# Fills of K on GpSimd, gates among the first maxima, and a reordered join between the stages of a two-layer network

## The chip, the cores and the metric

The kernel runs on one core of a Trainium2 chip. A core has five engines with queues of their own: TensorE (PE, matrix products and transposes), VectorE (DVE), ScalarE (ACT), GpSimd (POOL) and SyncE (SP, which here only issues transfers). The metric is the device time of one execution in microseconds (us). Time before: 1257.92 us, the median of three runs (1256.42 to 1259.0).

## The reference

The input is one sequence of 2048 tokens with 128 channels. Two layers follow each other. Each has an attention part and a feed-forward part, each in front of a gate and behind a layer norm whose scale and shift come from a small vector `c` through `wmod`:

```python
mod = (_silu(c) @ wmod).reshape(1, 6, 1, -1)
sa, ca, ga, sb, cb, gb = ...                       # six rows of 128
ga = (2 * (ga >= 0) - 1) * jnp.maximum(jnp.abs(ga), 0.25)      # gb alike
h = _layernorm(x) * (1 + ca) + sa;  x = x + ga * attention(h)
h = _layernorm(x) * (1 + cb) + sb;  x = x + gb * feed_forward(h)
```

- Layer 0's attention has 16 heads of 8 channels, with biases on all projections, and no mask.
- Layer 0's feed-forward adds a shared part (SiLU-gated, 512 wide) to the product of one expert of 16 per token, picked by the largest router logit and weighted by its sigmoid.
- Layer 1's attention has 8 query heads of 16 channels on one common key and value head, causal.
- Layer 1's feed-forward mixes each token with the one before it and gates a squared ReLU with a sigmoid.

## The kernel before

**Blocks.** The 2048 tokens lie in four query blocks of 512 (`QB`), each of four row tiles of 128 (`TB`). `x` stays in SBUF through both layers.

**Start.** `first_norm` normalises the four blocks: statistics on VectorE (L632, L633), the root on ScalarE (L635), the normalisation on VectorE (L228), four transposes on TensorE (L235) and the eviction with scale and shift on ScalarE (L236) into `hT`. Its PSUM pool is closed before the attention's is opened, so the attention's first product (`pq`, L676) needs the last eviction.

**Layer 0's attention.** A head's keys and queries are split into a high and a low half and stacked in rows, so that one product with 64 rows gives the score of two halves each. K's stack `kS0` has eight slices of 2048 columns. Each slice is first filled with a pattern (`fill`, L658: rows 31, 63, 95 and 127 are one, the others zero; the column `last_rows`, L97, holds it), then four transfers write the halves into part of its rows (`stack`, L259, from SP's queue, for the first two slices from ScalarE's too). The rows of ones serve to add the query's negative maximum to the score: the stack of queries gets that maximum in its rows 31, 63, 95 and 127.

**Units, two passes.** A unit is one query block and one group of four heads; there are 16. Its first pass (`first_pass`) makes 32 score tiles (L380, three PSUM buffers of 128 x 1024) and takes their maxima on VectorE (L384). At its end `largest` gathers the maxima (L395, L405, L406) and `turn` transposes them (L413), copies them (L414) and sends them into the query stack (L417). The second pass (`second_pass`) makes the scores again the other way round (L445), takes the exponential on ScalarE (L455) and weighs the values (L471).

**What sets the order.** The second pass of unit u and the first pass of the units after it are recorded alternately: `look_ahead` keeps the first passes a lead of `LEAD` = 8 steps in front. A turn waits in `turns` until two more steps are recorded. `late` holds pieces (normalising, projecting, routing) that are taken one at a time between the steps of a second pass; layer 0's list begins with `fold0`, which makes layer 1's modulation (L109) and gates (L121 to L126), folds gates into weights (L800, L802, L275, L277) and adds the output bias to `x` on GpSimd (L284). Up to the end of layer 0's attention a scheduler orders each engine's instructions from what is recorded; `keep_in_program_order` pins one of them.

**Join after layer 0's attention.** `last0` writes out an order by hand (from there on TensorE, VectorE and ScalarE keep the order of the program): the last projection, the shared part of the first block (`up` L869, `silu` L874, `times` L878, `down` L882, `add` L889), and the last block's routing (`choose`, `place`, `send`). `tiles` (L825 to L851) computes on VectorE which expert each tile of sorted tokens belongs to; SP's and TensorE's registers are loaded from its result `nth_i`, and SP then gathers the tokens (`xs`, L999).

**Experts, and the join before layer 1's attention.** Eight groups of expert tiles run with slices of the shared part of blocks 1 to 3 between them (`shared_step`: `shared_up` L972, `shared_act` L946 and L952, `shared_down` L960). After the last, tokens' expert rows are fetched by GpSimd (L1077) and added (L1091); blocks 0 and 1 are normalised (`moments`, L180 to L195, L228), and layer 1's keys and queries are made (L264).

Of the kernel before, what the change touches and what calls it, by code (L numbers as in the profile page):

```python
# [10 lines left out]
F32 = mybir.dt.float32  # L11
# [3 lines left out]
AF = mybir.ActivationFunctionType  # L15
# [28 lines left out]
def two_layers(ctx: ExitStack, tc: tile.TileContext, a: dict, out: bass.AP):  # L44
# [46 lines left out]
    def vcol(i, n=1):  # L91
        return vec[:, i:i + n]
# [3 lines left out]
    last_rows = const.tile([P, 1], F32, name="last_rows")  # L96
    nc.vector.tensor_reduce(last_rows, ident[:, 31::32], AX.X, ALU.add)  # L97

# [4 lines left out]

    def modulation(layer, ps):
        if layer == 0:
            nc.scalar.activation(sg, vcol(V_C0, 2), AF.Sigmoid)
            nc.vector.tensor_mul(sc, sg, vcol(V_C0, 2))
        for j in range(6):
            nc.tensor.matmul(ps[:, j:j + 1], wmod[layer][:, j * P:(j + 1) * P],  # L109
                             sc[:, layer:layer + 1], start=True, stop=True)  # L110
# [61 lines left out]

    def statistics(b, name):
# [9 lines left out]
        return mv, [lambda: some(0, TB // 2), lambda: some(TB // 2, TB)]  # L183

    def moments(b, name, root=False, between=lambda: None):


        mv, steps = statistics(b, name)
        for step in steps:
            step()  # L190
# [95 lines left out]
    def attention(layer, hT, ngrp, dk, scale, causal, kvp, begin, prepare, wq, bq, folded, ended,  # L286
# [23 lines left out]
        with ExitStack() as s:  # L310
# [36 lines left out]
            def project_q(b):  # L347
                if b in qS:
                    return
                ps = other_bank()  # L350
                nc.tensor.matmul(ps, wq, hT[:, b * QB:(b + 1) * QB], start=True, stop=True)
                hi = kvp.tile([P, QB], F32R, name=f"{L}qh{b}", tag="qh")
# [14 lines left out]
            def first_pass(u):  # L367
# [5 lines left out]
                def step(i, kb, pair):  # L373
# [9 lines left out]
                    if not own:  # L383
                        nc.vector.tensor_reduce(pm[:, i, 2 * pair:2 * pair + 2, kb], ps,  # L384
                                                AX.X, ALU.max)
                    for j in range(2 if own else 0):
# [37 lines left out]
                last = steps.pop()  # L424
                return steps + [lambda: (last(), largest(), turns.append([0, turn]))]

# [118 lines left out]
            shift, late, turns, weights, ready = {}, [], [], [], []  # L545
            if not folded:
                late.append(lambda: folded.extend(fold0(other_bank())))

            def all_first():
                for u in range(len(units)):  # L550
# [3 lines left out]
                    for i, step in enumerate(first_pass(u)):  # L554
# [3 lines left out]
                        if not fused and (grp, i) == (0, int(b > 0)) and b + 1 < NB:  # L558
                            ready.extend(prepare(b + 1, other_bank))
                            ready.insert(len(ready) - 1, lambda b=b: project_q(b + 1))  # L560
                        step()
                        if ready:
                            ready.pop(0)()
# [23 lines left out]

            short = 0 if fused else LEAD - 3
            look_ahead(ends[0] + LEAD - short)
# [66 lines left out]
    def fill(st):  # L656

        nc.scalar.activation(kS0[:, st, :], last_rows.to_broadcast([P, T]), AF.Copy)  # L658

# [5 lines left out]
    def begin0(ep, pp, stacks):  # L665
# [4 lines left out]
        vA = pool.tile([P, NT, (H0 - 1) * VW + W], F32, name="vA0", tag="vA")  # L670
        nc.gpsimd.memset(vA[:, :, H0 * VW:], 0.0)

        qhi = pool.tile([P, QB], F32R, name="a0qh0", tag="qh")
# [15 lines left out]
        for st in range(nst):  # L689
            rows = slice(st * 2 * D0, (st + 1) * 2 * D0)  # L690
            queues = (nc.sync, nc.scalar) if st < 2 else (nc.sync,)
            if st >= 2:
                fill(st)
            stack(kS[:, st, :], (hi[rows], lo[rows]), (0, 1, 0, 1), queues, RT // D0)
            stack(stacks[0][:, st, :], (qhi[rows], qlo[rows]), (0, 0, 1, 1), queues, RT // D0)
        for b in range(NB):
            for pair in range(TB // 2):
                ps = pp.tile([P, 2, QB], F32, name=f"pv{b}{pair}", tag="s")
                for j in range(2):
# [6 lines left out]
                    bv0.unsqueeze(1).to_broadcast([P, 2, H0 * VW]), ALU.add)  # L706
        gates(0)
        return ((lambda st: kS[:, st, :]),
                (lambda kt, head: vA[:, kt, head * VW:head * VW + W]), stacks[0])
# [113 lines left out]

    def tiles():

# [29 lines left out]
    def last0(late, bank, ps_s, ep):  # L855
# [41 lines left out]
        def rows():  # L897
# [30 lines left out]
    with ExitStack() as s:  # L928
# [159 lines left out]

        def add(b):
            ts = slice(b * TB, (b + 1) * TB)  # L1090
            return nc.vector.tensor_tensor(x[:, ts, :], x[:, ts, :], yx[:, ts, :], ALU.add)  # L1091
# [262 lines left out]
```

## Time and profile before

| | |
|---|---|
| Median of the runs | 1257.92 us (1256.42 to 1259.0) |
| The profiled execution | 1246.13 us, span 1244.4 us |
| TensorE busy | 1155.9 us, 93% of the span |
| VectorE busy | 951.9 us, 76% |
| ScalarE busy | 774.2 us, 62% |
| GpSimd busy | 85.9 us, 7% |
| Mean granted TensorE clock | 0.946 |

The span runs from the first to the last instruction of one execution. The rows by slice cut it into 40 equal parts of 31.1 us and give each engine's busy share in tenths. The chain of waits is followed back from the last instruction: each line has its start in us, its length in us, the engine, the tile written, the line of the kernel, and how many instructions it merges. A line of a group has engine, operation, output and input, shapes and count, then busy us and mean ns of one, then the idle time before it. A line of one tile's instructions gives the shortest, the middle and the longest duration in ns, and the first and last start.

### The profile page before, as it was taken

How to read it: one execution, taken by the hardware profiler on the slowest of the kernel's cores; microseconds unless marked ns; L12 is line 12 of the kernel's file. 1: busy time of each engine (PE TensorE's matmuls, PEld its weight loads, DVE VectorE, ACT ScalarE, POOL GpSimd, SP SyncE). 2: the span in 40 equal slices, each digit the busy share in tenths (PEclk: the TensorE clock that was granted, in tenths of full speed). 3: DMA queues.
4: the chain of work that ended last, by engine and by line, in shares of the span. 5: the costliest groups of instructions: out<-in, count | busy, mean ns of one | idle time of the engine just before them, and what ended most of it. 6: DMA issues, size and time to landing. Idle time of an engine off the chain costs nothing.

```text
span 1244.4 us, 22459 instructions
## 1 busy us (share of the span) xinstructions
PE 1155.9 (93%) x9264; PEld 527.9 (42%) x9264; DVE 951.9 (76%) x1515; ACT 774.2 (62%) x845; POOL 85.9 (7%) x152
## 2 busy tenths in 40 slices
PE   4679999999999999999999999979977999999995
PEld 2333433434443444343343443437744444444443
DVE  3788898899898889889889884243368699898532
ACT  6107777777777777777777778752333355656763
POOL 2002000000000000000000000230141111100111
PEclk9558999999999999999999999998987799999997
DMA  4841010202220212210000000032210101000000
GB/s 123 113 51 35 2 53 1 70 27 77 70 70 2 69 33 77 64 53 2 1 2 2 2 2 2 18 116 76 66 38 24 32 3 35 1 1 1 2 18 17
DMA packets 63110, 45.22 MB, mean 36 GB/s; under 512 B 6624, under 2 KB 56928, under 8 KB 62496
## 3 DMA queue, kind: packets, MB, share of 16 engines
q1 hardware_dynamic: 60240, 40.37, 13.2%
q10 hardware_dynamic: 1744, 1.32, 0.6%
q0 software_dynamic: 1024, 2.10, 0.6%
q8 instruction: 73, 1.20, 0.4%
q14 instruction: 29, 0.24, 0.1%
HBM read 9.88 MB, written 21.95 MB: 26 GB/s over the span
## 4 chain that ended last, share of the span: by engine, by line
PE 81%; DVE 12%; ACT 4%; DMA 1%; issue 1%; SPq 0%; DVEq 0%; ACTq 0%; POOLq 0%; POOL 0%
PE a0bank L471 24%; PE a0p L445 17%; PE a0p L380 13%; PE a1bank L471 5%; PE a1p L445 4%; DVE a0mx L384 3%; DVE a1mx L384 3%; PE a1p L380 2%; PE a1p L451 2%; DVE a1masked L389 2%; PE sg L972 2%; ACT a0e L455 1%; PE gu L1024 1%; PE a0bank L509 1%; PE sum L960 1%
## 5 line engine op out<-in xcount | busy, mean ns | idle before, releaser
L384 DVE TENSOR_REDUCE a0mx<-a0p 128x2 f32<-128x1024 f32 x512 | 623.8, 1224 | 74.6 <-PE a0p L380 64.9
L455 ACT ACTIVATE a0e<-a0p 128x1024 f32<-128x1024 f32 x512 | 522.6, 1025 | 171.5 <-PE a0p L445 146.4
L471 PE MATMUL a0bank<-a0e,vA 128*32 128x256 f32 x4096 | 333.3, 391 | 0.8 <-ACT a0e L455 0.8
L380 PE MATMUL a0p<-kS,a0qS 64*128 64x512 f32 x1024 | 248.0, 480 | 23.6 <-DVE a0mx L384 13.1
L445 PE MATMUL a0p<-a0qS,kS 64*128 64x512 f32 x1024 | 260.5, 497 | 0.0
L455 ACT ACTIVATE a1e<-a1p 128x1024 f32<-128x1024 f32 (+3 forms) x160 | 143.2, 897 | 108.5 <-PE a1p L451 103.0
L445 PEld LDWEIGHTS a0p<-a0qS,kS 64*128 64x128 f32 x1024 | 97.3, 184 | 204.5 <-issue 129.5
L380 PEld LDWEIGHTS a0p<-kS,a0qS 64*128 64x128 f32 x1024 | 100.3, 192 | 108.4 <-ACT a0e L455 56.8
L471 PEld LDWEIGHTS a0bank<-a0e,vA 128*32 128x32 f32 x4096 | 86.3, 108 | 137.4 <-issue 123.8
L384 DVE TENSOR_REDUCE a1mx<-a1p 128x2 f32<-128x1024 f32 x96 | 115.7, 1220 | 14.8 <-PE a1p L380 14.4
L471 PE MATMUL a1bank<-a1e,vA 128*32 128x256 f32 (+1 forms) x1152 | 97.1, 385 | 0.4 <-POOL a1e L458 0.4
L445 PE MATMUL a1p<-a1qS,kS 64*128 64x512 f32 (+3 forms) x320 | 76.6, 465 | 5.4 <-DVE a1mx L384 4.2
L380 PE MATMUL a1p<-kS,a1qS 64*128 64x512 f32 (+3 forms) x320 | 67.8, 423 | 11.5 <-DVE a1mx L389 4.6
L389 DVE CUSTOM_DVE_ANT_0 a1masked<-a1p,later 128x128 f32<-128x128 f32 (+3 forms) x128 | 62.4, 487 | 11.7 <-PE a1p L380 6.2
L780 POOL DMA_INDIRECT sent<-hs,row_i x16 | 15.8, 988 | 712.4 <-DVE ln11xn L228 689.2
L451 PE MATMUL a1p<-a1mT,a1ones 64*128 64x512 f32 (+3 forms) x320 | 61.7, 375 | 0.0
L445 PEld LDWEIGHTS a1p<-a1qS,kS 64*128 64x128 f32 x320 | 31.5, 189 | 63.3 <-issue 24.8
L380 PEld LDWEIGHTS a1p<-kS,a1qS 64*128 64x128 f32 x320 | 32.2, 195 | 39.9 <-DVE a1mx L389 11.6
L471 PEld LDWEIGHTS a1bank<-a1e,vA 128*32 128x32 f32 x1152 | 25.7, 108 | 42.5 <-issue 35.2
L458 POOL TENSOR_SCALAR_AFFINE_SELECT a1e<-a1e 128x256 f32<-128x256 f32 x64 | 26.1, 408 | 233.7 <-ACT a1e L455 233.7
L414 ACT CAST a0mT<-a0bank 8x512 fp32r<-8x512 f32 x16 | 9.2, 576 | 45.9 <-PE a0bank L413 45.9
L451 PEld LDWEIGHTS a1p<-a1mT,a1ones 64*128 64x128 f32 x320 | 32.0, 193 | 1.8 <-issue 1.3
(384 smaller groups left out, 718.2 us busy)
## 6 DMA issues: line engine op xcount, KB each, us to landing
sent<-blank SPq DMA_DIRECT2D x68, 256.0 KB
kS<-a0qS SPq DMA_DIRECT2D x28, 128.0 KB
wgu_sb<-in_gate_up SPq DMA_DIRECT2D x1, 2048.0 KB
a0qS<-a0qh SPq DMA_DIRECT2D x62, 32.0 KB
a0qS<-a0ql SPq DMA_DIRECT2D x62, 32.0 KB
xs<-sent SPq DMA_DIRECT2D x31, 64.0 KB
y_rows<-y SPq DMA_DIRECT2D x7, 256.0 KB
a1qS<-a1qh SPq DMA_DIRECT2D x24, 64.0 KB
```

What stands on the lines that cost most here:

```text
L380: nc.tensor.matmul(ps[:, j, :n], qS[b][r:r + RT, st, i * P:(i + 1) * P], kS(st)[r:r + RT, kb * QB:kb * QB + n], start=True, stop=True)
L384: nc.vector.tensor_reduce(pm[:, i, 2 * pair:2 * pair + 2, kb], ps, AX.X, ALU.max)
L389: nc.vector.tensor_tensor_reduce(masked[:, :n], ps[:, j, :n], later[:, QB - n:], 1.0, LOWEST, ALU.add, ALU.max, pm[:, i, g, kb:kb + 1])
L445: nc.tensor.matmul(ps[:, j, q0:], kS(st)[r:r + RT, kt * P:(kt + 1) * P], qS[b][r:r + RT, st, q0:], start=True, stop=fused)
L451: nc.tensor.matmul(ps[:, j, q0:], ones[r:r + RT, g // S, :], shift[u][r:r + RT, q0:], start=False, stop=True)
L455: nc.scalar.activation(e[:, :, q0:], ps[:, :, q0:], AF.Exp, scale=scale)
L458: nc.gpsimd.affine_select(out=e[:, :, q0:q0 + P], in_=e[:, :, q0:q0 + P], compare_op=ALU.is_ge, fill=0.0, base=0, pattern=[[0, 2], [1, P]] ...
L471: nc.tensor.matmul(av[g * W:(g + 1) * W, c0:c1], vA(kt, grp * HG + g), held[kt, g // 2][:, g % 2, c0:c1], start=(kt == 0 and c0 == 0), sto ...
L509: nc.tensor.transpose(ps[:, i * P:(i + 1) * P], o[:, i * P:(i + 1) * P], ident)
L780: nc.gpsimd.indirect_dma_start(out=sent[t], in_=hs[:, i, :], in_offset=None, out_offset=bass.IndirectOffsetOnAxis(ap=row_i.bitcast(U32)[:, ...
L960: nc.tensor.matmul(sums[b][:, i * P:(i + 1) * P], act[:, i * P:(i + 1) * P], wsd[:, k, :], start=(k == 0 and i == 0), stop=(k == NS - 1), ...
L972: nc.tensor.matmul(ps[:, j, :], w[:, k * P:(k + 1) * P], hT[:, b * QB:(b + 1) * QB], start=True, stop=True)
```

## The change

- `last_rows` is summed on GpSimd by three small additions instead of one reduction on VectorE.
- `fill` copies on GpSimd instead of ScalarE, and is pinned in the order of the program; the fills of slices 2 to 7 are recorded at the head of `begin0`, no longer between the transfers.
- `fold0` becomes three pieces, taken after the sixth, twelfth and eighteenth step of the first unit's first pass.
- The first unit's turn is taken at once; the first passes' lead starts at four and grows to eight during the first unit's second pass.
- A one-column exponential is recorded at the end of `begin0`.
- In `last0` the up-products are recorded ahead of their SiLU, and the products and down-products of slices 2 and 3 inside `tiles`.
- Before layer 1's attention the last two shared slices' up-products stand together ahead of the down-products; `x` gets the first block's expert rows tile by tile between the statistics; the last slice's product stands between the root and the reciprocal, its down-product ahead of layer 1's keys.

```diff
-    nc.vector.tensor_reduce(last_rows, ident[:, 31::32], AX.X, ALU.add)
+    nc.gpsimd.tensor_tensor(last_rows, ident[:, 31:32], ident[:, 63:64], ALU.add)
+    for i in (95, 127):
+        nc.gpsimd.tensor_tensor(last_rows, last_rows, ident[:, i:i + 1], ALU.add)
...
-    def moments(b, name, root=False, between=lambda: None):
+    def moments(b, name, root=False, between=lambda: None, before=lambda i: None):
-        mv, steps = statistics(b, name)
-        for step in steps:
+        mv, steps = statistics(b, name, TB)
+        for i, step in enumerate(steps):
+            before(i)
             step()
...
-                return steps + [lambda: (last(), largest(), turns.append([0, turn]))]
+                return steps + [lambda: (last(), largest(),
+                                         turns.append([2 if fused and u == 0 else 0, turn]))]
...
-            if not folded:
-                late.append(lambda: folded.extend(fold0(other_bank())))
+            folds = [] if folded else fold0(other_bank, folded)
...
                         step()
+                        if folds and i % 6 == 5:
+                            folds.pop(0)()
...
-            short = 0 if fused else LEAD - 3
+            short = LEAD - 4 if fused else LEAD - 3
...
     def fill(st):
-        nc.scalar.activation(kS0[:, st, :], last_rows.to_broadcast([P, T]), AF.Copy)
+        tc.keep_in_program_order(
+            nc.gpsimd.tensor_copy(kS0[:, st, :], last_rows.to_broadcast([P, T])))
...
         nc.gpsimd.memset(vA[:, :, H0 * VW:], 0.0)
+        for st in range(2, nst):
+            fill(st)
...
-            if st >= 2:
-                fill(st)
...
         gates(0)
+        t = lnp.tile([P, TB], F32, name="exptable", tag="y")
+        tc.keep_in_program_order(nc.scalar.activation(t[:, :1], eps, AF.Exp))
...
-    def fold0(bank):
-        modulation(1, bank)
-        gates(1)
-        nc.tensor.matmul(bank[:, :P], m[:, 5:6].to_broadcast([P, P]), ident, start=True, stop=True)
-        nc.scalar.copy(gb, bank[:, :P])
-        nc.gpsimd.tensor_tensor(wsd, wsd, gb.unsqueeze(1).to_broadcast([P, NS, P]), ALU.mult)
-        wog, rows = fold_gate(pool, bank, wo0, vcol(V_BO), m[:, 2:3], "a0")
-        for b in range(NB):
-            add_rows(b, rows)
-        return [wog]
+    def fold0(bank, folded):
+        def second():
+            modulation(1, bank(), tc.keep_in_program_order)
+            gates(1)
+        def first():
+            ps = bank()
+            nc.tensor.matmul(ps[:, :P], m[:, 5:6].to_broadcast([P, P]), ident, start=True,
+                             stop=True)
+            nc.scalar.copy(gb, ps[:, :P])
+            nc.gpsimd.tensor_tensor(wsd, wsd, gb.unsqueeze(1).to_broadcast([P, NS, P]), ALU.mult)
+        def fold():
+            wog, rows = fold_gate(pool, bank(), wo0, vcol(V_BO), m[:, 2:3], "a0")
+            for b in range(NB):
+                add_rows(b, rows)
+            folded.append(wog)
+        return [second, first, fold]
...
-    def tiles():
+    def tiles(between):
...
+        between(2)
         nc.vector.tensor_reduce(base, over, AX.X, ALU.add)
...
+        between(3)
         nc.vector.tensor_reduce(nth[:, 1, :SLOTS], passed[:, :, 1:], AX.X, ALU.add)
...
-                lambda: up(2, 0), lambda: silu(2), lambda: send(made[0]), lambda: ends_at(made[1]),
-                lambda: up(2, 1), lambda: up(3, 0), lambda: silu(3), lambda: up(3, 1), tiles,
-                lambda: times(2), lambda: down(2), lambda: times(3), lambda: down(3), add]
+                lambda: up(2, 0), lambda: up(2, 1), lambda: silu(2), lambda: send(made[0]),
+                lambda: ends_at(made[1]), lambda: up(3, 0), lambda: up(3, 1), lambda: silu(3),
+                lambda: tiles(lambda k: (times(k), down(k))), add]
...
-        while len(shared) > 1:
+        while len(shared) > 2:
             shared_step()
+        shared_act(*shared_up())()
         up = shared_up()
-        shared_down()
         last_times = shared_act(*up)
         table(AF.Sqrt)
-        add(0)
-        normed[0] = moments(0, "ln20", True)
+        shared_down()
+        shared_down()
+        normed[0] = moments(0, "ln20", True, last_times, lambda i: add(0, slice(i, i + 1)))
         norm(0)
         turn(0, bank)
-        last_times()
         add(1)
+        shared_down()
         normed[1] = moments(1, "ln21", True, lambda: keys(0, bank)())
...
         queries(1, q[1])
-        shared_down()
```

More of the change, by code (lines that the diff above doesn't have):

```diff
@@ L102, in two_layers, with modulation @@
     sc = const.tile([P, 2], F32, name="sc")
-    def modulation(layer, ps):
+    def modulation(layer, ps, place=lambda ins: ins):
         if layer == 0:
@@ L108, in modulation @@
         for j in range(6):
-            nc.tensor.matmul(ps[:, j:j + 1], wmod[layer][:, j * P:(j + 1) * P],
-                             sc[:, layer:layer + 1], start=True, stop=True)
+            place(nc.tensor.matmul(ps[:, j:j + 1], wmod[layer][:, j * P:(j + 1) * P],
+                                   sc[:, layer:layer + 1], start=True, stop=True))
         m = const.tile([P, 6], F32, name=f"mod{layer}", tag=f"mod{layer}")
@@ L171, in two_layers, with statistics @@
     lnp = ctx.enter_context(tc.tile_pool(name="lnp", bufs=2))
-    def statistics(b, name):
+    def statistics(b, name, parts=2):
         stats = lnp.tile([P, TB, nc.vector.BN_STATS_DIM], F32, name=name + "stats", tag="stats")
@@ L181, in some @@
                 nc.vector.bn_aggr(mv[:, i, :], stats[:, i, :])
-        return mv, [lambda: some(0, TB // 2), lambda: some(TB // 2, TB)]
-    def moments(b, name, root=False, between=lambda: None):
-        mv, steps = statistics(b, name)
-        for step in steps:
+        return mv, [lambda lo=lo: some(lo, lo + TB // parts) for lo in range(0, TB, TB // parts)]
+    def moments(b, name, root=False, between=lambda: None, before=lambda i: None):
+        mv, steps = statistics(b, name, TB)
+        for i, step in enumerate(steps):
+            before(i)
             step()
@@ L350, in project_q @@
                 ps = other_bank()
-                nc.tensor.matmul(ps, wq, hT[:, b * QB:(b + 1) * QB], start=True, stop=True)
+                product = nc.tensor.matmul(ps, wq, hT[:, b * QB:(b + 1) * QB], start=True,
+                                           stop=True)
+                if fused and b == 1:
+                    tc.keep_in_program_order(product)
                 hi = kvp.tile([P, QB], F32R, name=f"{L}qh{b}", tag="qh")
@@ L383, in step @@
                     if not own:
-                        nc.vector.tensor_reduce(pm[:, i, 2 * pair:2 * pair + 2, kb], ps,
-                                                AX.X, ALU.max)
+                        found = nc.vector.tensor_reduce(pm[:, i, 2 * pair:2 * pair + 2, kb], ps,
+                                                        AX.X, ALU.max)
+                        if fused and u == 1 and i == 0:
+                            tc.keep_in_program_order(found)
                     for j in range(2 if own else 0):
@@ L795, in two_layers @@
     gb = const.tile([P, P], F32, name="gb")
-    def fold0(bank):
-        modulation(1, bank)
-        gates(1)
-        nc.tensor.matmul(bank[:, :P], m[:, 5:6].to_broadcast([P, P]), ident, start=True, stop=True)
-        nc.scalar.copy(gb, bank[:, :P])
-        nc.gpsimd.tensor_tensor(wsd, wsd, gb.unsqueeze(1).to_broadcast([P, NS, P]), ALU.mult)
-        wog, rows = fold_gate(pool, bank, wo0, vcol(V_BO), m[:, 2:3], "a0")
-        for b in range(NB):
-            add_rows(b, rows)
-        return [wog]
+    def fold0(bank, folded):
[5 more added lines that the diff above has]
+            nc.tensor.matmul(ps[:, :P], m[:, 5:6].to_broadcast([P, P]), ident, start=True,
+                             stop=True)
+            nc.scalar.copy(gb, ps[:, :P])
[6 more added lines that the diff above has]
+        return [second, first, fold]
     folded1 = []
@@ L1087, in two_layers, with add @@
         normed = {}
-        def add(b):
-            ts = slice(b * TB, (b + 1) * TB)
+        def add(b, part=slice(0, TB)):
+            ts = slice(b * TB + part.start, b * TB + part.stop)
             return nc.vector.tensor_tensor(x[:, ts, :], x[:, ts, :], yx[:, ts, :], ALU.add)
```

## The prediction

> **What bounds the kernel now.** I read the engines' rows by slice first, then the chain of waits stretch by stretch, then the timeline of the stretches that the diff touches.
>
> ```profile
> PE   4679999999999999999999999979977999999995
> ACT  6107777777777777777777778752333355656763
> ```
>
> The TensorE (PE) row is full from the fourth slice (about 95 us) to the twenty-fifth. A windowed table gives it 198.8 of 200 us between 200 and 400 us, with VectorE (DVE) at 180.3. There only less matrix work would help, and TensorE's order of instructions is the same before and after from the end of the first unit's second pass to the last shared slices of the experts. So the change acts in three places: the first 145 us, the join after layer 0's attention (834 to 846 us), and the join before layer 1's attention (902 to 923 us). The chain of waits carries the first:
>
> ```profile
> 20.78 0.67 ACT hT L236
> 21.45 1.80 ACT kS L658
> 23.25 0.67 ACT hT L236
> 23.96 2.08 PE pq L676 x2
> ...
> 43.38 0.81 PE a0p L380 x2
> 44.21 36.29 DVE a0mx L384 x32
> ...
> 83.81 1.04 PE a0bank L413 x4
> ...
> 86.01 2.65 PE a0bank L109 x12
> ...
> 94.38 1.28 ACT L455
> 95.67 1.95 ACT a0e L455 x2
> ```
>
> The reader should see three things: ScalarE's fills of K (L658) stand between the normalised transposes (L236); the 32 maxima of the first unit run on VectorE alone, 1.13 us each; and 15.25 us pass between the last of these (80.42) and the first exponential (95.67), filled by the gates' products (L109 and what follows, TensorE 85.9 to 93.1) and by a table load of 1.28 us.
>
> **The change, part by part.** Times are on the profiled execution's clock (span 1244.4 us, 1246.13 with what lies around it).
>
> *Fills leave ScalarE.* Without them ScalarE's order is hT of block 0 at 13.4 (TensorE's transposes end then), the next root at 14.4, hT 1 at 15.25, hT 2 at 16.9 and hT 3 at 18.2 to 19.0, each 0.77 long and fed by VectorE's four normalisations (1.1 us per block). So the queries' product pq starts at 19.0, not 23.96. Before, the fill at 26.66 also held back K's high half (28.46); after, the low half ends at 19.0 + 8.5 = 27.5 instead of 33.37. K's transfers follow it, and so does the second maximum: 44.2 becomes 38.5. Gain if nothing else holds: 5.7.
>
> *Fills arrive on GpSimd.* Eight copies of 128x2048. No such copy is in the trace. Nearest rows:
>
> ```profile
> L336 POOL CAST a1ones<-a1onerows 128x256 fp32r<-128x256 f32 x1 | 0.4, 399 | 0.0
> L668 POOL MEMSET a0qS<- 128x4096 f32 x1 | 3.5, 3502 | 0.0
> ```
>
> At the memset's rate a fill takes 1.8 us; at the cast's (0.31 us more than 0.09 of start, per 256 columns) 2.56; at the two-input rate of L284 (1275 ns per 512) 5.0. The cast has the same operands, so I take 2.4. GpSimd's order is: first fill, then a mask that needs ScalarE's ones_r (now after hT 0, 14.4), second fill (14.9 to 17.3), memset of the stacked queries (3.5), a small memset (0.4), six fills, done near 36. The transfers of K that wait for each fill go out every 7 us, so even at 5.0 us per fill they find it done. The queries' transfers wait for the memset (20.9), needed at 21.8.
>
> The price lies elsewhere. VectorE's normalisations of blocks 2 and 3 now run while GpSimd is busy without a break. These rows show what that does:
>
> ```profile
> L228 DVE TENSOR_SCALAR ln20xn<-x,ln20mv,ln20y x4: 340/344/346, 909.6 to 910.5; 128x128 f32<-128x128 f32 x4
> L228 DVE TENSOR_SCALAR ln21xn<-x,ln21mv,ln21y x4: 335/337/652, 917.4 to 918.5; 128x128 f32<-128x128 f32 x4
> ```
>
> One of block 1's four took 652 ns: it began at 917.39, GpSimd's L284 ran from 916.67 to 917.95, and it ended 0.09 after that. [...] Block 2, ready at 15.5, waits for the second fill (17.3): 1.8. Its four go through together, the memset follows (to 21.9), and block 3 waits for it: 3.2. Cost 5.0, from 0 (no meeting) to 19 or so (below). The start's gain shrinks to 0.7.
>
> *Gates among the first maxima.* The products (2.72) now stand behind the sixth maximum. TensorE is at most three buffers ahead; it would start them at 4.2 us after the first maximum, finish at 6.9, and have the seventh score at 7.7 where VectorE wants it at 6.8: 0.95 lost. VectorE's 12 small instructions (1.0) and the folded weights (0.45) lie in its chain of maxima: +2.4 in all, 1.5 to 4. ScalarE's copies and GpSimd's additions lie beside it; GpSimd's come after its fills.
>
> *Shift turned at once, smaller lead, early table.* From the last maximum: three small reductions 0.55, transposes 1.1, copy 0.57, two transfers: 1.2 of issue and about 2 to land (an estimate from 2.2 to 2.5 us of the scattered rows), score 0.8: 6.2 us to the first exponential, against 15.25. Gain 9.05. Four score pairs less stand before it, and are owed during the pass: 4 x 0.34 = 1.4. The next block's query product (0.9 warm) moves from an idle TensorE at 19.7 into that pass. Owed 2.3. The cover of these steps on VectorE is thin: 36 maxima x 1.22 + 1.3 = 45.2 us, against TensorE's 32 x 1.0 + 36 x 0.34 + 0.9 = 45.1; up to 2 more. The shift's transfer is queued on SP behind the stacked K; that queue ended 7.3 us before it, and keeps 6.7.
>
> First place: -0.7 + 2.4 - 9.05 + 2.3 = -5.05.
>
> *Rows before layer 1, second place.*
>
> ```profile
> 838.77 0.64 DVE nth L849
> 839.82 0.61 DVE s0act L878
> 840.47 3.79 PE s0ps L882 x16
> 844.29 0.70 DVE x L889
> 845.03 5.94 PE sg L972 x8
> ```
>
> VectorE's list of tiles runs to 839.8 while TensorE stands, then two products (0.65 each), 16 matmuls and an addition follow. After, both products stand inside the list, with all four up-products done by 836: the list ends at 839.8 + 1.3 = 841.1, the matmuls lie under it, the addition ends 841.85, and the next products start 841.95 instead of 845.03. Gain 3.1. The list's numbers come 1.3 later, so do 31 gathers on SP (842.5 to 843.8); the first four are needed at 851.7 and land near 848. The eight products at 0.74 each are at half the rate of later ones (1.72 for four): if TensorE's clock stays up, 2.5 more. Range 0 to 5.6.
>
> *Last shared slices, third place.*
>
> ```profile
> 905.31 1.73 PE sg L972 x4
> 907.07 0.60 ACT sigs L946
> 907.67 1.28 ACT L1141
> ...
> 917.67 1.03 PE sum L960 x8
> ```
>
> The last up-product comes 0.9 earlier, so the table load does; but VectorE's four split additions cost 2.65 instead of 0.68 + 1.7, and the last product (0.68) now stands ahead of the reciprocal. The normalisation starts 0.3 earlier. The sum at 917.67 goes into the wait for hT: 1.0. Gain 1.2 (-1 to 2.5).
>
> Total: -5.05 - 3.1 - 1.2 = -9.4. The profiled execution is 11.8 below the median of the runs shown (1257.92), and nothing here explains that; I let the difference carry over: 1248.5.
>
> **The rivals.**
>
> [...]
>
> *No meeting.* The scalars' form escapes, or the fills come at another moment: 5.0 less, 1243.5. Against it stands the 652 ns row.
>
> *Gains swallowed by the small lead.* With four scores ahead, not eight, TensorE's order alternates between waiting for a maximum and for an exponential; 0.25 us in each of 32 steps takes 8 of the first place's gain: 1256.5, no change that can be told. For it: VectorE and TensorE are equal to 0.1 us in that pass; against: at a lead of eight the same two ran at 90% and 99%.
>
> **How the numbers follow.** Two holds 0.40 (own range 1245 to 1252), no meeting 0.27, alternating 0.20, swallowed 0.13. A change of 0.2% (2.5 us) is about what a measurement of this kernel can tell from none. Faster: 0.40 + 0.27 + half of swallowed's spread, 0.06; same 0.06; slower 0.21. Range 1240 to 1262.5: from no meeting with the warm clock to alternating; longer fills (5.0 us each while alternating, +17 more) and the best ends together are left out.
>
> **What would show it.** pq's product: at 19 no meeting, 24 two holds, 38 alternating; a normalisation of 1.5 to 3 us in VectorE's rows; fills on GpSimd at 2.4 us each; the first exponential 6 us after the last of the first 32 maxima; TensorE's sg products 3 us earlier relative to the hs product; no wait for K's transfers after the fifth pair. The prediction is wrong if a fill takes over 4 us and holds VectorE, or if the first unit's second pass is longer than before by over 5 us.

## The result, and the profile after

The changed kernel is slower: 1264.53 us (median of six runs, 1261.86 to 1266.11) against 1257.53 us before (six runs), 1.0055 times before with a 95% interval of 1.004 to 1.007. The forecast was 1248.5 us. Measured once more beside three other kernels it took 1261.79 us against 1257.34, 1.0046 (1.003 to 1.0062).

The profiled execution took 1263.0 us (span 1261.3). That is 16.9 us more than the profiled execution of before, while the medians differ by 7.0. Chips differ: on one the kernel before has a median of 1246.12 us, on two others 1257.28 and 1257.34. The profiled execution of before, from which the forecast was read, is as fast as those of the first chip; on which chip it ran is not on record. A large part of the gap is one pause at the third place (last section). So times are compared with the kernel before on the same chip. The first place is little touched by this: in two profiles each, the first unit's division, with which its second pass ends, comes at 144.81 and 144.00 us in the kernel before, and at 153.39 and 155.32 in the changed one.

The chain of waits of the changed kernel, over the stretch shown of before (start in us, length in us, engine, tile, line, instructions merged):

```profile
14.99 8.98 DVE ln02xn L231 x4
...
25.80 6.46 DVE ln03xn L231 x3
...
33.03 0.79 ACT hT L239
...
33.86 2.07 PE pq L689 x2
...
53.65 2.37 DVE a0mx L390 x2
...
74.90 15.84 DVE a0mx L390 x14
...
91.10 2.21 DVE a0nm L413
...
93.66 1.10 PE a0bank L421 x4
...
96.08 1.80 DMA a0qS<-a0mT
...
98.01 0.80 PE a0p L454 x2
```

ScalarE's fills are gone from the chain, as they should be, yet pq starts at 33.86 us, not 23.96. In front of it stand the normalisations of blocks 2 and 3 with 8.98 and 6.46 us. One tile's instructions (shortest, middle and longest in ns, first and last start):

```profile
L231 DVE TENSOR_SCALAR ln02xn<-x,ln0mv,ln0rstd x4: 1903/2930/5253, 15.0 to 22.1; 128x128 f32<-128x128 f32 x4
L231 DVE TENSOR_SCALAR ln03xn<-x,ln0mv,ln0rstd x4: 1076/1920/2847, 25.7 to 31.2; 128x128 f32<-128x128 f32 x4
```

Before, block 2's four took 341 to 346 ns each. The timeline of the same stretch, GpSimd's lines among VectorE's (start, length of the group, engine, line, operation, output and input, count):

```profile
14.48 1.89 POOL L669 CAST kS<-last_rows 128x2048 fp32r<-128x2048 f32 x1
...
14.99 8.98 DVE L231 TENSOR_SCALAR ln02xn<-x,ln0mv,ln0rstd 128x128 f32<-128x128 f32 x4
...
16.31 3.51 POOL L679 MEMSET a0qS<- 128x4096 f32 x1
19.75 0.41 POOL L682 MEMSET vA<- 128x368 f32 x1
20.11 11.12 POOL L669 CAST kS<-last_rows 128x2048 fp32r<-128x2048 f32 x6
...
23.98 1.76 DVE L128 TENSOR_TENSOR mod<-sign,mag 128x1 f32<-128x1 f32 x1
...
25.72 6.59 DVE L231 TENSOR_SCALAR ln03xn<-x,ln0mv,ln0rstd 128x128 f32<-128x128 f32 x4
31.19 0.98 POOL L344 MEMSET a0nm<- 128x512 f32 x2
```

GpSimd works without a gap from 14.5 to 32.2 us, and in that time nine held instructions of VectorE get through: four normalisations, one 128x1 product, four normalisations. They end at 20.24 and 20.31, 22.13, 23.97, 25.74, 27.64, 29.48, 32.25 and 32.31 us. Where one fill follows another, one instruction passes at each end of a fill (it ends 0.01 to 0.08 us after it). Where a clearing follows, none ends until the clearings are over (at 20.16 and 32.17), and then two end together; the second of the two is recorded as starting when the fill ends (at 16.36 and at 31.24). GpSimd starts its run this late because the strict mask (L163) rewrites the tile of ones that ScalarE copies first (L162), so it waits until 14.18 us. The clearing of the query stack (L679) ran from 4.56 to 8.06 us before; recorded behind the pinned second fill, it now stands behind that mask too.

A second meeting lies at the end of the first unit's maxima, in the timelines of VectorE and GpSimd:

```profile
91.10 2.20 DVE L413 CAST a0nm<-a0nx 128x16 fp32r<-128x16 f32 x1
```

```profile
89.76 3.51 POOL L364 MEMSET a0qS<- 128x4096 f32 x1 [9.49 <-DMA a0qS<-a0ql]
```

A cast of 128x16 took 2.20 us (0.16 before) and ended 0.03 us after GpSimd's clearing of the second query stack. Before, that clearing ran at 98.74 us, behind the gates' additions, past the cast; with the gates moved forward it is free earlier and meets the one VectorE instruction that everything waits for.

### The profile page after: what moved, and what is told of

Same layout as the page of the kernel before. It is cut to its first block, busy times and chain, and to the rows that moved or that the text cites. A ratio compares the mean times of both kernels' runs of the same rounds, so it can differ in the third digit from the quotient of the medians.

```text
span 1261.3 us, 22471 instructions
## 1 busy us (share of the span) xinstructions
PE 1153.7 (91%) x9264; PEld 525.9 (42%) x9264; DVE 968.0 (77%) x1517; ACT 759.7 (60%) x838; POOL 101.5 (8%) x163
## 4 chain that ended last, share of the span: by engine, by line
PE 79%; DVE 13%; ACT 3%; issue 1%; DMA 1%; another core or an unknown queue 1%; SPq 0%; DVEq 0%; ACTq 0%; POOLq 0%; POOL 0%
PE a0bank L480 23%; PE a0p L454 17%; PE a0p L386 12%; PE a1bank L480 5%; PE a1p L454 4%; DVE a1mx L390 3%; DVE a0mx L390 3%; PE a1p L386 2%; PE a1p L460 2%; DVE a1masked L397 2%; ACT a0e L464 1%; PE sg L997 1%; PE gu L1049 1%; PE a0bank L518 1%
## 5 line engine op out<-in xcount | busy, mean ns | idle before, releaser
L480 PEld LDWEIGHTS a0bank<-a0e,vA 128*32 128x32 f32 x4096 | 86.8, 108 | 139.8 <-issue 124.5
L390 DVE TENSOR_REDUCE a1mx<-a1p 128x2 f32<-128x1024 f32 x96 | 115.8, 1221 | 14.5 <-PE a1p L386 14.1
```

What stands on the lines that cost most here:

```text
L390: found = nc.vector.tensor_reduce(pm[:, i, 2 * pair:2 * pair + 2, kb], ps, AX.X, ALU.max)
L480: nc.tensor.matmul(av[g * W:(g + 1) * W, c0:c1], vA(kt, grp * HG + g), held[kt, g // 2][:, g % 2, c0:c1], start=(kt == 0 and c0 == 0), sto ...
```

## The experiments

All kernels compute the whole result. All but the first were timed in turn with the kernel before on the same chip; the ratios are to that, and need not equal the quotient of the two medians (they can differ by 0.002, or some 2 us). The interval behind a ratio is at 95%.

**The kernel before, profiled again.** No edit.

> The kernel before, unchanged, profiled once more. Its first profiled execution took 1246.13 us while its other runs took 1256.3 to 1259.0. If the pause that the changed kernel's profile shows at the third place (10.6 us of ScalarE and 8.6 us of VectorE idle until 929.1, while the token gathers finish) belongs to most executions of both kernels and was only missing from that first profile, this profile takes 1255 to 1259 us and shows such a pause between 909 and 925. If the pause is made by the change, this profile takes 1245 to 1248 us again and shows none.

1251.78 us in its profiled execution; the eleven runs of before on that chip have a median of 1257.28. The time fell between the two ranges, but the profile shows the pause. Its longest waits without a named releaser:

```profile
ACT hT L236 <- remote: 7.0, 1, 7.0
ACT sigs L946 <- remote: 5.0, 1, 5.0
```

So the pause is no work of the change. The first profile of before is without it.

**The fills back on ScalarE and between the transfers, all else as changed.**

```diff
-        tc.keep_in_program_order(
-            nc.gpsimd.tensor_copy(kS0[:, st, :], last_rows.to_broadcast([P, T])))
+        nc.scalar.activation(kS0[:, st, :], last_rows.to_broadcast([P, T]), AF.Copy)
...
-        for st in range(2, nst):
-            fill(st)
...
             queues = (nc.sync, nc.scalar) if st < 2 else (nc.sync,)
+            if st >= 2:
+                fill(st)
```

> The changed kernel with the eight fills back on ScalarE and everything else left as changed (last_rows still from GpSimd, so that the first two fills can start early). If GpSimd's fills and clearing alternate with VectorE's normalisations, the normalisations of blocks 2 and 3 take 0.34 us each again instead of 2 us, the q product starts at 20 to 24 us instead of 33.9, and the time falls by 10 to 14 us against the changed kernel, to 1250 to 1255 us. If the loss comes from the other edits of the first place (gates among the maxima, smaller lead) the start is earlier but the end of the first place is not, and the time stays within 3 us of 1264.5.

1248.38 us against 1257.28: 0.9945 (0.9924 to 0.9966). Block 2's normalisations take 339 to 346 ns, pq starts at 22.5 us. The time is a little below the range. Taking the fills off GpSimd turns the change from a loss into a gain.

**Only the fills moved, all else as before.**

```diff
+        tc.keep_in_program_order(
+            nc.gpsimd.tensor_copy(kS0[:, st, :], last_rows.to_broadcast([P, T])))
-        nc.scalar.activation(kS0[:, st, :], last_rows.to_broadcast([P, T]), AF.Copy)
...
         nc.gpsimd.memset(vA[:, :, H0 * VW:], 0.0)
+        for st in range(2, nst):
+            fill(st)
```

> The kernel before with only the fills (and the one column they copy) moved to GpSimd. Alternation: q product at 33 to 35 us instead of 24.0, 9 to 10 us lost in the first place and kept to the end: 1266 to 1268 us. My forecast's reading (two holds of 5.0 us in all, against 5.7 us of ScalarE freed): q product at 23, time 1256 to 1258 us.

1268.22 us against 1257.28: 1.0086 (1.0062 to 1.0111), 10.9 us lost (0.2 above the range), pq at 34.9 us. That is more than the whole change loses; the other edits together gain.

**The fills on GpSimd, but out of the way.** The mask gets a tile of its own, the clearing of the query stack is pinned behind the second fill, and the last six fills read a copy of the column that VectorE makes after its last normalisation.

```diff
-    nc.gpsimd.affine_select(out=ones_f, in_=ones_f, compare_op=ALU.is_gt, fill=0.0,
+    strict = const.tile([P, P], F32, name="strict")
+    nc.gpsimd.memset(strict, 1.0)
+    nc.gpsimd.affine_select(out=strict, in_=strict, compare_op=ALU.is_gt, fill=0.0,
...
-        nc.gpsimd.memset(stacks[0].bitcast(F32), 0.0)
+        tc.keep_in_program_order(nc.gpsimd.memset(stacks[0].bitcast(F32), 0.0))
...
+        rows = const.tile([P, 1], F32, name="rows_late")
+        tc.keep_in_program_order(nc.vector.tensor_copy(rows, last_rows))
         for st in range(2, nst):
-            fill(st)
+            fill(st, rows)
```

> The changed kernel with GpSimd's big writes kept apart from the normalisations: the strict mask is built in a tile of its own, so that the second fill and the clearing of the q stack no longer wait behind a ScalarE copy until 14.2 us, and the last six fills copy a column that VectorE makes only after its last normalisation. Alternation as the cause: normalisations of 0.34 us except one or two that meet the clearing, q product at 19 to 21 us, 12 to 14 us less than the changed kernel, 1250 to 1253 us. If the cost is that GpSimd does the fills at all, wherever they stand: no earlier than 30 us, time within 3 us of 1264.5.

1247.35 us against 1257.28: 0.9939 (0.9916 to 0.9962), below the range. Its normalisations:

```profile
L233 DVE TENSOR_SCALAR ln02xn<-x,ln0mv,ln0rstd x4: 341/342/347, 16.7 to 17.4; 128x128 f32<-128x128 f32 x4
L233 DVE TENSOR_SCALAR ln03xn<-x,ln0mv,ln0rstd x4: 342/344/347, 18.0 to 18.7; 128x128 f32<-128x128 f32 x4
```

GpSimd does the same eight fills, and pq starts at 20.5 us. Where they stand is what costs. Beside the changed kernel itself the same kernel came to:

> The changed kernel with the fills out of the normalisations' way, once more, beside the changed kernel itself. Alternation as the cause of the whole loss: 13 to 15 us less than the changed kernel in the same runs, 0.994 times before.

1250.78 us against 1261.79 for the changed kernel and 1257.34 before: 0.994 (0.9919 to 0.9961), 11.0 us below the changed kernel, short of the 13 to 15 expected.

**Each fill in two halves, the clearing in eight parts, in the changed kernel's places.**

```diff
-        tc.keep_in_program_order(
-            nc.gpsimd.tensor_copy(kS0[:, st, :], last_rows.to_broadcast([P, T])))
+        for lo in range(0, T, T // 2):
+            tc.keep_in_program_order(
+                nc.gpsimd.tensor_copy(kS0[:, st, lo:lo + T // 2],
+                                      last_rows.to_broadcast([P, T // 2])))
...
-        nc.gpsimd.memset(stacks[0].bitcast(F32), 0.0)
+        for st in range(nst):
+            tc.keep_in_program_order(nc.gpsimd.memset(stacks[0].bitcast(F32)[:, st, :], 0.0))
```

> The changed kernel with each fill as two instructions of half the width and the clearing as eight of an eighth, in the same places: as much for GpSimd to write, in 24 pieces. If each normalisation waits for one instruction of GpSimd (one for one), it waits some 0.45 to 1 us instead of 1.9 and gets through before the fills end: q product at 24 to 28 us instead of 33.9, the time 6 to 10 us less than the changed kernel. If the normalisations wait until GpSimd's writing is done, or only share a rate with it, the number of pieces doesn't matter: q product at 33 to 35 us and the changed kernel's time.

1255.13 us, 6.7 us below the changed kernel on the same chip, 0.9989 times before (0.9978 to 1.0001); pq at 28.2 us, at the edge of the range. Its timeline:

```profile
14.63 3.00 POOL L670 CAST kS<-last_rows 128x1024 fp32r<-128x1024 f32 x3
15.14 6.73 DVE L231 TENSOR_SCALAR ln02xn<-x,ln0mv,ln0rstd 128x128 f32<-128x128 f32 x4
17.58 3.78 POOL L682 MEMSET a0qS<- 128x512 f32 x8
...
21.68 11.93 POOL L670 CAST kS<-last_rows 128x1024 fp32r<-128x1024 f32 x12
22.76 4.02 DVE L231 TENSOR_SCALAR ln03xn<-x,ln0mv,ln0rstd 128x128 f32<-128x128 f32 x4
```

A half fill starts every 0.99 us, and block 3's four normalisations take 1.06 to 1.07 us each: one per half fill. Block 3 is through at 26.8 us while GpSimd writes on until 33.6, so VectorE does not wait for the writing to be done. The eight parts of the clearing gave nothing: block 2's third normalisation stood from 16.65 to 21.81 us, through a half fill and all the clearings, as in the changed kernel.

**The join after layer 0's attention put back**, in the kernel with the fills out of the way.

```diff
-                lambda: up(2, 0), lambda: up(2, 1), lambda: silu(2), lambda: send(made[0]),
-                lambda: ends_at(made[1]), lambda: up(3, 0), lambda: up(3, 1), lambda: silu(3),
-                lambda: tiles(lambda k: (times(k), down(k))), add]
+                lambda: up(2, 0), lambda: silu(2), lambda: send(made[0]), lambda: ends_at(made[1]),
+                lambda: up(2, 1), lambda: up(3, 0), lambda: silu(3), lambda: up(3, 1),
+                lambda: tiles(lambda k: None),
+                lambda: times(2), lambda: down(2), lambda: times(3), lambda: down(3), add]
```

> The kernel of the run with the fills out of the way (1247.35 us), with the join after layer 0's attention put back in the order of before. My forecast held this part to gain 3.1 us (0 to 5.6): 1250.5 us (1247.3 to 1253). If the part gains nothing: 1246 to 1248.5 us.

1238.52 us against 1246.12 (this chip is the fast one): 0.9941 (0.9923 to 0.996). The numbers of the expectation are for the other chip, as in the next three; as a ratio it read 0.9965 if the part gains 3.1 us, 0.994 if it gains nothing. No gain is seen, also beside the late-gather kernel below (1238.25 us, same chip, the join as changed); but each of the intervals reaches some 2 us to either side. The profiles say where the gain went. From block 2's normalisation in layer 0's second norm (ln12xn) to the first before layer 1 (ln20xn), the late-gather kernel needs 104.5 us and this one 107.7: 3.2 us gained, as the forecast had it. From ln20xn to ln22xn they need 54.0 and 50.7: given back. The windowed rows (window; length; busy us of PE, PEld, DVE, ACT and POOL; granted clock; DMA share; GB/s) of the late-gather kernel, and then of this one:

```profile
911.00:923.00 12.00, 9.95 (x32) 4.90 (x30) 7.45 (x29) 4.70 (x7) 7.90 (x8) 0.61 0.18 43
```

```profile
913.00:925.00 12.00, 7.69 (x37) 3.64 (x36) 10.40 (x38) 4.93 (x8) 1.26 (x1) 1.00 0.11 28
```

TensorE's granted clock was 0.61 there against 1.00, and 32 matrix instructions kept it busy for 9.95 us there, 37 for 7.69 here. The two other profiles from this chip with the join as changed agree: 104.3 and 104.5 us for the first stretch, 54.8 and 52.9 for the second; in the first of them, with the last shared slices put back, the clock was 0.77 from 909 to 921 us. With the join put back there is one profile. Why the clock differed was not tried.

**The last shared slices put back**, in the same kernel.

```diff
-        while len(shared) > 2:
+        while len(shared) > 1:
             shared_step()
-        shared_act(*shared_up())()
         up = shared_up()
+        shared_down()
         last_times = shared_act(*up)
         table(AF.Sqrt)
-        shared_down()
-        shared_down()
-        normed[0] = moments(0, "ln20", True, last_times, lambda i: add(0, slice(i, i + 1)))
+        add(0)
+        normed[0] = moments(0, "ln20", True)
...
+        last_times()
         add(1)
-        shared_down()
         normed[1] = moments(1, "ln21", True, lambda: keys(0, bank)())
...
+        shared_down()
```

> The same kernel with the last shared slices and the moments of blocks 0 and 1 put back in the order of before. My forecast held this part to gain 1.2 us (2.5 lost to 1 gained at the ends): 1248.5 us. The rival from the profiles: in the changed order the profiles show one pause of 10 us at this place and in the order of before two of together 12 us, both ending when the last token gathers land, so the order hardly matters: 1246 to 1249.5 us. If the changed order makes the pause longer, this kernel is the faster: 1240 to 1245 us.

1240.16 us, 0.9955 (0.9939 to 0.997). Against the late-gather kernel on the same chip (1238.25, 0.992 to 0.995), which has the changed order but differs in its gathers too, the changed order is 1.9 us ahead, with intervals that overlap: the forecast's 1.2 us is neither confirmed nor excluded.

**The full lead of eight**, in the same kernel.

```diff
-            short = LEAD - 4 if fused else LEAD - 3
+            short = 0 if fused else LEAD - 3
```

> The same kernel with the scores of unit 0 starting eight steps behind the maxima again instead of four. My forecast: the lead of four is worth 4.9 us less 2.3 us that is owed later, so this kernel takes 1250 us. The rival (what the smaller lead gains at the start is paid back while the maxima catch up): 1246.5 to 1248.5 us, with unit 0's division at the same time within 1 us although the first exponentials start some 5 us later.

1235.62 us, 0.9919 (0.9894 to 0.9944): the smaller lead shows no gain. The first exponential starts at 88.7 us instead of 85.8 to 86.8 in the three other kernels on this chip, and yet the first unit's division comes at 139.7 instead of 140.2 to 141.4.

**The last eight gathers later**, in the same kernel.

```diff
-        for t in range(NT):
+        gather(range(2 * TB))
...
+        late = pool1.tile([P, NT], I32, name="late_slots")
+        nc.vector.tensor_copy(late[:, 2 * TB:], slot_i[:, 2 * TB:])
+        gather(range(2 * TB, NT), late)
         table(AF.Exp)
```

> The same kernel with the last eight of the sixteen token gathers issued only after the third place (they copy their slots from a tile that VectorE writes there). If the 10 us pause of the engines that wait for TensorE lasts until the last gather lands, it ends when the eighth lands, or is short: the third place becomes 5 to 10 us shorter and the time 1238 to 1243 us. If the pause has nothing to do with the gathers it stays at 8 to 10 us: 1246 to 1250 us.

1238.25 us, 0.9935 (0.992 to 0.995). Inconclusive on the pause: this chip shows none in any of its four profiles, with the gathers early or late.

**The changed kernel again**, on the chip of the half fills.

> The changed kernel unchanged, on the chip of the three runs after it. Its first comparison gave 1.0055 times before. If the pause at the third place, which showed on one chip in both kernels and on another chip in none, is the same in both, the ratio stays at 1.004 to 1.008. If the changed order makes it longer or shorter, a chip without the pause gives 1.000 to 1.003 or over 1.009.

1.0046 (1.003 to 1.0062), with the pause (10.7 us on ScalarE) in its profile. What it would be on a chip without the pause was not measured.

**The pieces together**: the kernel with the fills out of the way, with the clearing and the second fill after the last normalisation too (the first stays early), and the full lead.

```diff
-            short = LEAD - 4 if fused else LEAD - 3
+            short = 0 if fused else LEAD - 3
...
-    for st in range(2):
-        fill(st)
+    fill(0)
     first_norm()
...
+        after = const.tile([P, 1], F32, name="after_norm")
+        tc.keep_in_program_order(nc.gpsimd.tensor_copy(after, rows))
+        tc.keep_in_program_order(nc.gpsimd.memset(stacks[0].bitcast(F32), 0.0))
...
-        for st in range(2, nst):
-            fill(st)
+        for st in range(1, nst):
+            fill(st, rows)
```

> The fills out of the way, with the full lead of eight, and with the clearing of the q stack and the second fill after the last normalisation too, so that block 0's normalisation isn't held from 11.5 to 13.2 us. If the pieces add: q product at 18.5 to 19.5 us instead of 20.5, 1 to 4 us less than the kernel with the fills out of the way, 0.990 to 0.993 times before. If the start is no longer what sets the first place, no better than 0.994.

1251.08 us against 1257.34: 0.9943 (0.9921 to 0.9964), no better than the kernel with the fills out of the way. pq starts at 19.4 us, 1.1 earlier: the product of two columns in front of layer 0's modulation takes 0.14 us, where it took 1.26 during the second fill. The first unit's maxima are copied 2.0 us earlier (79.8 against 81.8), but its division comes at 140.6 against 140.0. In these profiles the start no longer sets the end of the first unit. The versions with the fills out of the way are 0.5 to 0.8% faster than the kernel before, and more than the changed one.

## Why the prediction was wrong

The step that failed is the cost of VectorE's normalisations meeting GpSimd's writes. The forecast had two holds: "Its four go through together, the memset follows (to 21.9), and block 3 waits for it: 3.2. Cost 5.0". No run shows these 5.0 us, nor the 19 at the upper end: they were my estimate, with one row of 652 ns behind the wait and nothing behind the four that go through together. What the changed kernel shows is a hold of 14.5 us: pq at 33.86 against the 19.37 of the kernel in whose start nothing meets. The four do not go through together. Each held instruction ends 0.01 to 0.08 us after one of GpSimd's, the second of a pair 0.15. At each of five ends of a fill, from 22.05 to 29.40 us, one instruction of VectorE gets through; while the two clearings ran, from 16.31 to 20.16, none did. On GpSimd's side no wait is seen: its fills start every 1.84 us here, and every 1.83 in the last kernel, where the normalisations are over. Half the size takes the hold of one from 1.9 to 1.07 us, which is the direct test of one for one.

In kind this is what the forecast calls alternating, with pq at 38: one instruction of VectorE gets through at each end of one of GpSimd's. It was given 0.20 because the trace of before had no case of a queued one. It had one pass behind a clearing too, where none did, and took a fill at 2.4 us. The fill, costed between 1.8 and 5.0, took 1.88 us (the eight: 1.879 to 1.936).

The first place, term by term, from the profiles of before and after. One reading of before has to be put right first. The 32 maxima that the chain of waits has from 44.21 us begin with the second of the first unit and so end with the first of the next unit:

```profile
40.48 1.23 DVE L384 TENSOR_REDUCE a0mx<-a0p 128x2 f32<-128x1024 f32 x1 [2.18 <-PE a0p L380]
44.21 36.29 DVE L384 TENSOR_REDUCE a0mx<-a0p 128x2 f32<-128x1024 f32 x32 [2.51 <-PE a0p L380]
```

The first unit's last maximum therefore ended one maximum (1.13 us) before the end of this row, at 79.37, and from there to the first exponential it is 16.30 us, not 15.25. In the changed kernel the unit's last maximum ends at 90.75 with none of the next unit's before the cast.

| Term | Forecast | Measured |
|---|---|---|
| Start, at the second maximum | -0.7 | +9.4 (44.21 to 53.65) |
| Gates among the maxima | +2.4 | +1.9 (second maximum to the end of the last: 35.2 to 37.1) |
| Last maximum to first exponential | -9.05 | -8.2 (16.30 to 8.10) |
| Owed in the first unit's pass | +2.3 | +5.4 (first exponential to division: 49.14 to 54.54) |
| Sum | -5.05 | +8.6 (division at 144.81 and 153.39) |

- *Fills leave ScalarE*: right. pq was to start at 19.0 without a meeting; it did at 19.4.
- *Gates*: within the forecast's range. But the move had a price that I put nowhere: GpSimd's clearing of the next query stack came forward with it and held the 128x16 cast for 2.0 us. The kernel with the fills out of the way still pays it (the cast takes 2.32 us in its profile).
- *Shift at once*: 6.2 us were forecast from the last maximum; 8.10 were measured, which are 6.1 and that hold.
- *Owed*: mis-sized by 3.1 us. A first unit's pass over 5 us longer was one of the forecast's own signs of being wrong, and "Gains swallowed by the small lead" was the right rival for this term. The full lead brings the pass back to 51.0 us, and of the 2 to 3 us that it starts later nothing is left at the division.
- *Second place*: the 3.1 us are there (3.2 in the pair of profiles), but are not seen in the time. The forecast stopped at the join and took what lies behind it as shifted along. In the changed kernel's own profile the stretch from ln12xn to ln20xn shows no gain (108.5 us before, 108.8 after): from ln12xn to ln13xn, ahead of the join, 4.8 us are lost (25.9 to 30.7), and from there on 4.5 gained (82.6 to 78.1). The granted clock was 0.50 from 830 to 836 us (1.00 before). By an estimate from these figures that accounts for at most 3 of the 4.8, half of the 6 us; the rest was not traced.
- *Third place*: 1.2 us forecast, 1.9 measured between overlapping intervals.

How this makes the whole: the forecast's gain of 9.4, which has 5.0 of holding in it, breaks even at a hold of 14.4 us, and 14.5 were measured, so the hold alone takes that gain to nothing. What makes it a loss in the profiles is chiefly the 3.1 us more that are owed. The first place's +8.6 with the forecast's -3.1 and -1.2 makes +4.3, without them +8.6; the medians differ by 4.5 and 7.0.

How much the rest of the change gains is not settled. Only the fills moved costs 10.9 us, so behind the held start the rest gains some 4 to 6.5, less than the 8.7 us that the forecast gave it (its -9.4 with the -0.7 of the start taken out). The owed maxima, the second hold and the join's missing gain are candidates for the difference. But with the fills back on ScalarE, where the pass is as long (55.05 us), the medians are 8.9 us apart, which by the ratio (0.9945) is 6.9.

## What to carry to other kernels

Before work is moved to GpSimd, list what VectorE runs in the same stretch and whether it reads and writes SBUF in the forms seen here to be held; then count one GpSimd copy for each of VectorE's instructions (1.9 us each beside the fills here), and a row of clearings as a whole (3.86 us here). Either keep the two engines apart with a small data dependency (pq at 20.5 us instead of 33.86) or cut GpSimd's copies small (28.2 at half the size); cutting the clearing gave nothing here. Mind what stands behind a wait: here one mask that waited for ScalarE until 14.18 us put a clearing of 3.5 us beside the normalisations. And a stage that only shifts its start earlier is worth what is left at the end of the next stage; the smaller lead and the last 1.1 us of earlier start that were tried here left nothing.

## What the runs showed of the hardware

**What was held, and what was not.** Held in the changed kernel while GpSimd wrote: normalisations (128x128, SBUF to SBUF, 1.08 to 5.25 us instead of 0.34), a product of two SBUF columns (128x1, 1.76 instead of 0.15), a cast (128x16, 2.20 instead of 0.16), so small instructions as well as large ones. Not held, in the kernel with the fills out of the way: statistics (0.26 to 0.30 us, during a fill and during the clearing), and the low half's instruction with PSUM input (128x512, 0.75 us at 23.3, amid six fills). The clearings of the changed kernel held the normalisations (one from 14.99 to 20.24) and the cast (from 91.10 to 93.30), but that of the last kernel did not hold a product of two columns (0.16 us at 18.3, 0.1 us into the clearing).

**A pause that two chips show and a third does not.** At the third place of the changed kernel ScalarE and VectorE stood until 929.1 us, though TensorE's work that they wait for is recorded as over at 921.3. ScalarE's timeline, then VectorE's, then GpSimd's last gather:

```profile
918.20 0.30 ACT L196 ACTIVATE ln20y<-ln20mv,eps 128x4 f32<-128x4 f32 x1 [0.43 <-issue]
929.10 0.78 ACT L239 ACTIVATE hT<-a1bank,mod 128x512 f32<-128x512 f32 x1 [10.60 <-remote]
```

```profile
929.19 0.69 DVE L990 TENSOR_TENSOR x<-x,sum 128x512 f32<-128x512 f32 x1 [8.60 <-remote]
```

```profile
925.46 0.94 POOL L1102 DMA_INDIRECT yx<-y_rows,slot_i  x1 [0.30 <-issue]
```

The same eviction in the kernel with the join put back, on the chip without the pause:

```profile
906.66 0.78 ACT L241 ACTIVATE hT<-a1bank,mod 128x512 f32<-128x512 f32 x1 [2.28 <-PE a1bank L240]
```

The pause is in all nine other profiles, the first of before left out: eight from two chips, and the changed kernel's first, whose chip is not on record. It lasts 3.5 to 10.7 us at this eviction, with up to 8.5 more ahead of it where the order is that of before, and in all nine it ends 3.2 to 4.1 us after the issue of the last gather begins. In the four profiles of the fast chip, and in the first one of before, it is absent; in those with the gathers in their usual place the eviction starts 3.8 to 4.3 us before the last gather is issued. Between the two profiles of before, with the pause and without, the stretch from ln12xn to ln21xn is 8.2 us longer (124.5 against 116.3), while the executions differ by 5.7 us and the medians of the chips by 11.2. So the pause is a large part of the gap between the chips, not shown to be all of it. That the gathers cause it was not shown either: the run meant for it fell on a chip without the pause.
